# Moving the fetch of the next x, two centred tiles and the splitting units in a hand-ordered retention and FFN kernel

## The chip, the core and the metric

The kernel runs on one core of one Trainium2 chip. A core has five engines with a queue each: TensorE (PE, matmuls; its weight loads are listed as PEld), VectorE (DVE), ScalarE (ACT), GpSimd (POOL) and SyncE (SP, which here issues nearly all DMAs). Each works through its queue in order and waits for the others by semaphores. The metric is the device time of one execution in microseconds; lower is better.

## The reference

Input x has 4 sequences of 1024 tokens with 512 features. Two sublayers follow one another, each with a layer norm before it and one after it, and added to its input:

```python
def attn(x):                                   # x is already normed
    q = x @ Wq.T;  v = x @ Wv.T                # 512 x 512 each
    ret = scan(v)                              # state = lam * state + v_t along the tokens, lam per head
    out = layernorm(q * ret) * gamma + beta
    return (out * silu(x @ Wg.T)) @ Wo.T

def ffn(x):                                    # weights rounded to fp8, I = 1536
    return ((silu((x @ gate_w) * gate_scale) * ((x @ up_w) * up_scale)) @ down_w) * down_scale

x = x + layernorm(attn(layernorm(x)))
x = x + layernorm(ffn(layernorm(x)))
```

All is in float32, and the kernel keeps that precision: operands are either multiplied as float32 or split into parts [...].

## The kernel before

The 4096 tokens are worked in 8 blocks of 512 tokens (t = 0 to 7), a block in 4 tiles of 128 tokens (s = 0 to 3). The main loop (line 1223) runs over blocks, and within a block over 12 steps (line 1226, i = 0 to 11), one for each 128 of the 1536 hidden columns. Every step holds the FFN of block t: `f.gate(i)` (8 matmuls into pfg, read by ACT), `f.up(i)` (8 matmuls into pfu), `f.fuse(i)` (DVE's gate product, then ACT's cast), `f.rest(i)` one step later (DVE), and `f.down(i - 2)` (8 matmuls into pd). Gate and up share two PSUM banks in turn, so that up(i+1) waits until DVE has read up(i).

Between these, by hand, stand three other pieces of work: `l`, the FFN before, being normed and stored (steps 2 to 4); `b`, the attention of block t+1; and `n`, the preparation of block t+2 (an object `Retention`, made at the end of step 4). Every engine's order is the order of the program text (class InOrder, line 66), so where a call stands in the loop body decides behind what it queues on its engine. Within a step the body runs, from line 1228 to 1541: before the gate, between gate and up, after fuse ("mid" below, around line 1381), and after down ("end", around line 1531).

Attention of a block comes in two kinds. Blocks 2 and 3 (`fast`) use seven products instead of eight of half-sized operands for each of v, q, g and o (`product`, line 650; `order`, line 333). Blocks 4 to 7 (`by_parts`) split x and the weights into a top and a low part and use three passes for v, q and g (`begin`, `end`, lines 590 and 597, placed by `gaps`, line 458), and products for o. The weights of all these are not held: they stream through a ring of four slots, and after each product or pass one fetch of 256 KB is issued on SP for the unit four places on (`fetch_weights`, line 435).

What the change touches:

- Preparing x of block t+2, for by_parts blocks (n.t = 4 to 7, so t = 2 to 5). Tile s is normed (`norm_x`, line 504, ACT), transposed in blocks of 32 (DVE) and written to DRAM (`send_x`, line 523, SP): tile 0 at the end of step 6, 1 and 2 at the end of step 7, 3 at the mid of step 8. It is read back in the wanted layout by four DMAs a tile (`fetch_x`, line 539): tile 0 in step 7, 1 to 3 in step 8. Then `low_of` (line 555: two DVE operations, top and low) and `diff_of` (line 570: one) make the parts: low 0 in step 8, low 1 and 2 in step 9 before up, diff 0, 1 and 2 in step 9 mid, low 3 and diff 3 in step 10 mid. The first use on PE is `n.gap(-2)` in step 11 (line 1340): the top pass, then the low pass, which needs the low parts of all four tiles.
- The second norm of block t+1 (`b`). The o products give mids; `o_moments` (statistics on DVE, rstd on POOL), `x1_of` (line 901: three ACT operations, POOL's addition to x, a store), `x1_moments`, `x1n_of` (line 912: centre and scale). Tiles 0 and 1 are centred in step 9 (lines 1360 to 1366), by DVE for blocks 2 and later (`center_scale`, line 273), and transposed by DVE and DMAs (`move_x1n`); tiles 2 and 3 are centred in steps 10 and 11 by DVE and transposed on PE (`turn_x1n`, lines 1494 and 1497).
- The splitting units (class Splitter, line 388), in blocks 1 and 2: twelve units of 256 KB of Wv, Wq and Wg are loaded, split by three DVE operations and one POOL operation, and the parts are stored in DRAM for the by_parts blocks. One load of two units at the end of step 0 of block 1, then one unit a step in steps 1, 3, 4, 5, 8, 9 of block 1 and 0 to 5 of block 2 (line 1227), always loading at the mid and storing at the end.
- The sums of Wo (`output_sums`, line 371; `keep_sums`, line 383) at the end of step 0 of block 1: three plain quarters are stored to DRAM, four sums made on DVE in the same place and stored.

## Time and profile before

| | before |
|---|---|
| median of 3 timed runs (range) | 990.18 us (989.87 to 992.27) |
| the profiled execution, whole | 991.58 us |
| its span, first to last instruction | 989.8 us |
| PE busy | 954.3 us (96%) |
| DVE, ACT, POOL busy | 679.1, 427.3, 273.0 us |
| mean granted TensorE clock | 0.992 |
| start of the loop's block 0, 1, 2, 3, 4, 5, 6, 7 | 94.7, 197.8, 323.4, 449.1, 568.0, 685.3, 804.5, 915.0 us |

In the profile's lines an instruction is named by engine, operation and out<-in tiles: pfg, pfu and pd are gate, up and down; pv, pq, pg and po the attention's products; pt a transpose on PE; mids the attention's sums; st and mv statistics; split_room the splitting units. An idle stretch of an engine stands in brackets with what ended it. All instructions carry one line number (L74), that of the helper that keeps the order, so they are told apart by tiles. The row of a window gives the busy time of PE, PEld, DVE, ACT and POOL with the number of instructions, then the granted TensorE clock as a share of full speed (PEclk), the DMA share and GB/s.

### The profile page before, as it was taken

Reading aid. Unit: us, or ns where it says so; the run is one execution under the profiler, and the core shown is the slowest. Engines: PE = TensorE matmul, PEld = TensorE weight load, DVE = VectorE, ACT = ScalarE, POOL = GpSimd, SP = SyncE. Lnnn points to the kernel's source line nnn. Section 1 sums busy time; section 2 is a strip of 40 time slices with the busy share of each in tenths; the row PEclk is TensorE's granted clock in tenths of the full one; section 3 lists DMA queues with packets and bytes.
Section 4 is the critical chain, followed back from the end, with each engine's and each line's share of the span. In section 5 each row is a group of like instructions: output and inputs, shape, how many; then the busy total and the mean of one; then the engine's idle time right before and its main releaser. Section 6 shows DMA issues by size and latency. Waiting matters only on the chain.

```text
span 989.8 us, 11929 instructions
## 1 busy us (share of the span) xinstructions
PE 954.3 (96%) x4022; PEld 748.0 (76%) x4022; DVE 679.1 (69%) x1054; ACT 427.3 (43%) x673; POOL 273.0 (28%) x340
## 2 busy tenths in 40 slices
PE   9999999999999999989999899998999999999997
PEld 7456766777877878768878688886878778788885
DVE  5996998767768788674675845867457755647444
ACT  3546674467555125332353324433163332624223
POOL 1405212404327043140332305222052311414020
PEclk9999999999999999999999999999999999999999
DMA  9312324864738557455455465455454454424021
GB/s 296 119 64 69 123 65 111 268 200 153 226 116 244 177 171 261 153 155 179 150 170 155 128 186 149 162 156 177 144 174 153 135 181 145 148 64 125 4 86 42
DMA packets 115500, 148.14 MB, mean 150 GB/s; under 512 B 10864, under 2 KB 60016, under 8 KB 115440
## 3 DMA queue, kind: packets, MB, share of 16 engines
q1 hardware_dynamic: 114576, 146.73, 47.8%
q8 instruction: 32, 0.52, 0.3%
q10 hardware_dynamic: 864, 0.66, 0.2%
q14 instruction: 28, 0.23, 0.1%
HBM read 108.02 MB, written 42.47 MB: 152 GB/s over the span
## 4 chain that ended last, share of the span: by engine, by line
PE 38%; DVE 8%; POOL 4%; ACT 3%; issue 3%; DMA 1%; SPq 0%; DVEq 0%; POOLq 0%; ACTq 0%
PE pd L74 8%; PE pfg L74 8%; PE pfu L74 8%; PE pv L74 4%; PE po L74 4%; PE pq L74 3%; PE pg L74 2%; DVE st L74 2%; DMA kept<-x 1%; POOL x L74 1%; POOL d L74 1%; ACT x1n L74 1%; DVE diff L74 1%; DVE low L74 1%; POOL mvd L74 1%
## 5 line engine op out<-in xcount | busy, mean ns | idle before, releaser
L74 PE MATMUL pfu<-x1nT,up_sb 128*128 128x512 f32 x768 | 201.6, 405 | 5.5 <-DVE gate L74 5.5
L74 PE MATMUL pfg<-x1nT,gate_sb 128*128 128x512 f32 x768 | 194.7, 395 | 0.1
L74 PE MATMUL pd<-down_sb,fuse 128*128 128x512 f32 x720 | 186.0, 400 | 0.0
L74 PEld LDWEIGHTS pfu<-x1nT,up_sb 128*128 128x128 f32 x768 | 144.6, 189 | 41.0 <-DVE gate L74 8.6
L74 PEld LDWEIGHTS pfg<-x1nT,gate_sb 128*128 128x128 f32 x768 | 144.0, 188 | 30.4 <-DVE x1nT L74 0.8
L74 PEld LDWEIGHTS pd<-down_sb,fuse 128*128 128x128 f32 x720 | 136.8, 190 | 28.5
L74 ACT CAST fuse<-gate 128x512 fp32r<-128x512 f32 x90 | 55.6, 618 | 183.5 <-DVE gate L74 183.5
L74 DVE SCALAR_TENSOR_TENSOR gate<-pfu,us_sb,gate 128x512 f32<-128x512 f32 x96 | 71.8, 748 | 59.6 <-PE pfu L74 53.6
L74 ACT ACTIVATE gate<-pfg,gs_sb 128x512 f32<-128x512 f32 x96 | 65.6, 684 | 105.4 <-PE pfg L74 105.3
L74 POOL TENSOR_SCALAR mv<-mv 128x1 f32<-128x1 f32 (+1 forms) x82 | 23.8, 290 | 253.0 <-DVE mv L74 249.9
L74 DVE TENSOR_TENSOR fuse<-gate,fuse 128x512 fp32r<-128x512 f32 x90 | 73.9, 821 | 5.5 <-ACT fuse L74 5.5
L74 DVE BATCH_NORM_STATS2 st<-x 128x6 f32<-128x512 f32 x64 | 43.6, 681 | 25.3 <-POOL x L74 22.6
L74 POOL TENSOR_TENSOR ysum<-y 128x512 f32<-128x512 f32 (+1 forms) x10 | 12.0, 1202 | 156.8 <-DVE y L74 156.7
L74 POOL TENSOR_TENSOR mv<-mv,nhalf 128x1 f32<-128x1 f32 (+1 forms) x75 | 50.9, 679 | 6.2
L74 DVE TENSOR_TENSOR mids<-po,mids 128x512 f32<-128x512 f32 x30 | 20.5, 684 | 36.4 <-PE po L74 36.3
L74 POOL TENSOR_TENSOR x<-x,x1n 128x512 f32<-128x512 f32 x32 | 41.5, 1298 | 12.7 <-ACT x1n L74 12.0
L74 POOL TENSOR_TENSOR d<-d,x 128x512 f32<-128x512 f32 x28 | 36.2, 1317 | 16.1 <-ACT d L74 14.1
L74 POOL TENSOR_TENSOR sqsum<-sqsum,sq 128x512 f32<-128x512 f32 x24 | 35.1, 1464 | 14.9 <-ACT sq L74 13.5
L74 POOL TENSOR_TENSOR ysum<-ysum,y 128x512 f32<-128x512 f32 (+1 forms) x20 | 23.1, 1157 | 54.3 <-DVE y L74 54.0
L74 DVE TENSOR_TENSOR y<-pq,y 128x512 f32<-128x512 f32 x18 | 12.4, 691 | 35.7 <-PE pq L74 35.7
L74 POOL TENSOR_SCALAR split_room<-split_room 128x512 f32<-128x512 f32 x12 | 9.5, 788 | 93.2 <-DVE split_room L74 93.2
L74 DVE RECIPROCAL rstd<-rstd 128x512 f32<-128x512 f32 x8 | 26.8, 3352 | 11.8 <-ACT rstd L74 11.8
(199 smaller groups left out, 1636.6 us busy)
## 6 DMA issues: line engine op xcount, KB each, us to landing
kept<-x SPq DMA_DIRECT2D x32, 256.0 KB, 2.1
x<-kept SPq DMA_DIRECT2D x32, 256.0 KB, 4.3
x<-in_x SPq DMA_DIRECT2D x28, 256.0 KB, 4.5
w_ring_parts<-dsum_o SPq DMA_DIRECT2D x28, 256.0 KB, 2.7
out<-d SPq DMA_DIRECT2D x27, 256.0 KB, 2.0
xnT<-mx SPq DMA_DIRECT2D x64, 64.0 KB, 2.0
w_ring_parts<-dtop_v SPq DMA_DIRECT2D x16, 256.0 KB, 2.9
w_ring_parts<-dlow_v SPq DMA_DIRECT2D x16, 256.0 KB, 2.9
```

The costliest lines, as they stand in the source:

```text
L74: return lambda *args, **kwargs: tc.keep_in_program_order(op(*args, **kwargs))
```

## The change

Seven edits, all in where things stand:

1. For by_parts blocks, x tile 1 is normed and sent in step 7 before up, tile 2 at the mid of step 7 and tile 3 at the end of step 7. The fetch is by pairs: tiles 0 and 1 in step 7 mid, tiles 2 and 3 in step 8 before up.
2. low 0 and 1 move to step 8 before up, low 2 and 3 to the end of step 8.
3. diff 0 and 1 move to step 9 before up, diff 2 and 3 to step 10 mid, after x1n of tile 2.
4. x1n of tiles 0 and 1 in step 9 is centred on ACT (`shift_scale`, line 276: two operations on one column, one on the tile) in every fast block, so for t = 1 to 6.
5. The splitting units get a table of load (l), split (s) and store (k) by block, step and place. Units 0 to 4 are split in block 1 (steps 2, 3, 4, 8, 9), 5 to 11 in block 2 (two in step 0, two in step 1, one each in steps 2, 3, 4); none in step 5. Unit 7 uses another buffer.
6. The plain quarters of Wo are no longer stored and read back: products of blocks 2 and 3 fetch them from the input, and at the end of step 10 of block 1 they are copied from DRAM to DRAM for the later blocks.
7. The four sums of Wo are stored at the end of step 1 of block 1 instead of step 0, and the first two unit loads follow there.

```diff
@@ -370,16 +370,23 @@
 
     def output_sums():
 
+        v = woT.rearrange("(c p) f -> p c f", p=P)
+        operands["o"] = {1: v[:, 0:2, 0:H], 2: v[:, 2:4, 0:H], 3: v[:, 2:4, H:D]}
         b11, b12, b21, b22 = (wo_sb[:, i : i + 2, o : o + H] for i in (0, 2) for o in (0, H))
-        operands["o"] = {}
-        made["o"] = {1: b11, 2: b21, 3: b22}
-        keep_sums("o")
         made["o"] = {5: b11, 7: b12, 6: b22, 4: b21}
         dve.tensor_tensor(b11, b12, b11, ALU.subtract)
         dve.tensor_tensor(b12, b22, b12, ALU.subtract)
         dve.tensor_tensor(b22, b22, b11, ALU.subtract)
         dve.tensor_tensor(b21, b21, b22, ALU.subtract)
 
+    def copy_output_weights():
+
+        operands["late o"] = dict(operands["o"])
+        for j in (1, 2, 3):
+            t = dram.tile([P, 2, H], F32, tag=f"sum_o{j}", name=f"dcopy_o{j}", bufs=1)
+            sp.dma_start(t, operands["o"][j])
+            operands["late o"][j] = t
+
     def keep_sums(k):
         for j, t in made[k].items():
             operands[k][j] = dram.tile([P, 2, H], F32, tag=f"sum_{k}{j}", name=f"dsum_{k}{j}", bufs=1)
@@ -389,44 +396,51 @@
         def __init__(self):
-            self.room = wpool.tile([P, 4, D], F32, tag="wo_sb", name="split_room")
+            room = wpool.tile([P, 4, D], F32, tag="wo_sb", name="split_room")
+            self.pairs = [(room[:, 0], room[:, 1]), (room[:, 2], room[:, 3])]
...
-            self.loaded = self.done = self.kept = 0
-
-        def of(self, n):
+            self.pair = {n: p if p is None else self.pairs[p] for n, p in enumerate((0, 1, 0, 1, 0, 1, 0, None, 1, 0, 1, 0))}
+
+        def load(self, n):
...
+            if self.pair[n] is None:
+                room = work.tile([P, 2, D], F32, tag="xn", name=f"split_room_{n}", bufs=1)
+                self.pair[n] = room[:, 0], room[:, 1]
...
+        times = {
+            (1, 1, "end"): "l0 l1", (1, 2, "mid"): "s0", (1, 2, "end"): "k0", (1, 3, "mid"): "l2 s1",
+            (1, 3, "end"): "k1", (1, 4, "mid"): "l3 s2", (1, 4, "end"): "k2", (1, 5, "mid"): "l4",
+            (1, 8, "mid"): "s3", (1, 8, "end"): "k3", (1, 9, "mid"): "l5 s4", (1, 9, "end"): "k4",
+            (1, 10, "mid"): "l6", (2, 0, "mid"): "l7 s5", (2, 0, "end"): "k5 s6", (2, 1, "mid"): "l8 s7 k6",
+            (2, 1, "end"): "l9 s8", (2, 2, "mid"): "k7 k8 s9", (2, 2, "end"): "l10 k9", (2, 3, "mid"): "l11 s10",
+            (2, 3, "end"): "k10", (2, 4, "mid"): "s11", (2, 4, "end"): "k11",
+        }
+
+        def at(self, *when):
+            do = {"l": self.load, "s": self.split, "k": self.store}
+            for what in self.times.get(when, "").split():
+                do[what[0]](int(what[1:]))
@@ -443,7 +457,8 @@
         ring = rings[n >= change].bitcast(F32)[:, n % RING]
         what = stream[n]
         if len(what) == 2:
-            unit = operands[what[0]][what[1]]
+            k, j = what
+            unit = operands["late o" if k == "o" and n >= change else k][j]
             sp.dma_start(ring.rearrange("p (c f) -> p c f", c=2), unit)
         else:
             sp.dma_start(ring, operands[what[:2]][what[2]])
@@ -538,7 +553,7 @@
 
         def fetch_x(self, s=None):
             xnT = self.xnT.bitcast(F32)
-            tokens, groups = (slice(None), slice(None)) if s is None else (ts(s, P), ts(s, P // Q))
+            tokens, groups = (slice(None), slice(None)) if s is None else (ts(s, 2 * P), ts(s, 2 * P // Q))
             for a in range(NQ):
                 sp.dma_start(
                     xnT[ts(a, Q), groups].rearrange("p g c j -> p g (c j)"),
@@ -1224,7 +1239,6 @@
         f, n = Ffn(a), None
         fast = b is not None and b.fast
         for i in range(NI):
-            splits = (t == 1 and i in (1, 3, 4, 5, 8, 9)) or (t == 2 and i < 6)
             if t > 0 and (t > 1 or i) and not (fast and i == 11):
                 (f if i else l).rest((i - 1) % NI)
             if t == 0 and i == 0:
@@ -1272,9 +1286,16 @@
                 b.gap(3 * i)
             if fast and 7 <= i < 10:
                 b.product()
-            if n and n.by_parts and i in (8, 9):
-                for s in ([0], [1, 2])[i - 8]:
-                    n.low_of(s)
+            if n and n.by_parts and i == 7:
+                n.norm_x(1, True)
+                n.send_x(1)
+            if n and n.by_parts and i == 8:
+                n.fetch_x(1)
+                n.low_of(0)
+                n.low_of(1)
+            if n and n.by_parts and i == 9:
+                n.diff_of(0)
+                n.diff_of(1)
             if t == PARTS - 2 and i == 9:
                 for _ in range(RING - 1):
                     fetch_weights()
@@ -1354,19 +1375,14 @@
                 n.input_sums(*((3, 4) if fast else (1, 2)))
             if t == 0 and i == 11:
                 b.upper_of(2)
-            if n and n.by_parts and i == 9:
-                n.diff_of(0)
-                n.diff_of(1)
             if fast and i == 9:
                 loads = []
                 for s in range(2):
-                    b.x1n_of(s)
+                    b.x1n_of(s, shift_scale)
                     loads.append(b.move_x1n(s))
                 for load in loads:
                     load()
-                if n and n.by_parts:
-                    n.diff_of(2)
-                elif n:
+                if n and not n.by_parts:
                     n.input_sums(1, 2)
             if fast and i == 11:
                 for s in range(2):
@@ -1378,9 +1394,6 @@
                 next(passing)
             if fast and i < 6:
                 b.gap(3 * i + 1, 2 if i == 1 else 1)
-            if splits:
-                splitter.load()
-                splitter.split()
             if fast and i == 2:
                 l.stats(1)
             if fast and i == 3:
@@ -1400,18 +1413,20 @@
                 b.gate_y(0)
                 b.gate_y(1)
                 b.y_sums(1, 2)
-            if n and n.by_parts and i == 8:
-                n.fetch_x(1)
-                n.fetch_x(2)
-            if n and t > 0 and i == 8:
+            if (1, 0) < (t, i) < (2, NI):
+                splitter.at(t, i, "mid")
+            if n and t > 0 and i == 8 and not n.by_parts:
                 n.norm_x(3, True)
                 n.send_x(3)
             if n and n.by_parts and i == 7:
                 n.fetch_x(0)
             if fast and i in (7, 8):
                 b.product()
-            if n and t > 0 and i == 8:
-                n.fetch_x(3 if n.by_parts else None)
+            if n and n.by_parts and i == 7:
+                n.norm_x(2, True)
+                n.send_x(2)
+            if n and t > 0 and i == 8 and not n.by_parts:
+                n.fetch_x()
             if fast and i == 8:
                 b.o_moments(0)
                 b.o_moments(1)
@@ -1423,10 +1438,9 @@
             if fast and i == 10:
                 b.x1_moments(2)
                 b.x1_moments(3)
-                if n and n.by_parts:
-                    n.low_of(3)
                 b.x1n_of(2)
                 if n and n.by_parts:
+                    n.diff_of(2)
                     n.diff_of(3)
             if t == 0:
                 if i == 3:
@@ -1455,7 +1469,7 @@
             if b and not fast and i >= 9:
                 b.rest_of(i - 9)
             if n and t > 0 and i in (6, 7):
-                for s in ([0], [1, 2])[i - 6]:
+                for s in ([0], [3] if n.by_parts else [1, 2])[i - 6]:
                     n.norm_x(s, True)
                     n.send_x(s)
             for _ in range(look[i][1] if t == 1 else 0):
@@ -1503,6 +1517,9 @@
                 b.gap(3 * i + 2)
             if fast and i in (7, 8):
                 b.product()
+            if n and n.by_parts and i == 8:
+                n.low_of(2)
+                n.low_of(3)
             if fast and i == 2:
                 l.stats(2)
             if fast and i == 3:
@@ -1524,12 +1541,13 @@
                 n.stats(1)
             if t == 1 and i == 0:
                 output_sums()
+                splitter = Splitter()
+            if t == 1 and i == 1:
                 keep_sums("o")
-                splitter = Splitter()
-                splitter.load()
-                splitter.load()
-            if splits:
-                splitter.store()
+            if t == 1 and i == 10:
+                copy_output_weights()
+            if (1, 0) < (t, i) < (2, NI):
+                splitter.at(t, i, "end")
             if t == 0 and i == 10:
                 t_sums = wpool.tile([P, 4, 2, H], F32, tag="wq_sb", name="t_sums")
                 mids = wpool.tile([P, 4, 2, H], F32, tag="wg_sb", name="mids")
```

More of the change, by code (lines that the diff above doesn't have):

```diff
@@ L398, in of @@
+        def load(self, n):
             k, c = self.units[n]
-            w, top = self.room[:, 2 * (n % 2)], self.room[:, 2 * (n % 2) + 1]
-            return k, c, w, top
-        def load(self):
-            n = self.loaded
-            if n < len(self.units) and n - self.kept < 2:
-                self.loaded += 1
-                k, c, w, _ = self.of(n)
-                src = self.sources[k].rearrange("(c p) f -> p c f", p=P)[:, :, ts(c, P)]
-                sp.dma_start(w.rearrange("p (c f) -> p c f", c=NC), src)
-                parts = operands[k, c] = {
-                    part: dram.tile([P, D], F32, tag=f"{part}_{k}{c}", name=f"d{part}_{k}{c}", bufs=1)
-                    for part in ("top", "low", "diff")
-                }
-                sp.dma_start(parts["top"].rearrange("p (c f) -> p c f", c=NC), src)
@@ L415, in split @@
-        def split(self):
-            if self.done < self.loaded:
-                _, _, w, top = self.of(self.done)
-                dve.tensor_scalar(top.bitcast(I32), w.bitcast(I32), TOP_MASK, None, ALU.bitwise_and)
-                dve.tensor_tensor(w, w, top, ALU.subtract)
-                dve.scalar_tensor_tensor(top, top, -LOW, w, ALU.mult, ALU.add)
-                pool.tensor_scalar(w, w, 1.0 / LOW, 1.0, ALU.mult, ALU.mult)
-                self.done += 1
-        def store(self):
-            while self.kept < self.done:
-                k, c, w, top = self.of(self.kept)
-                sp.dma_start(operands[k, c]["diff"], top)
-                sp.dma_start(operands[k, c]["low"], w)
-                self.kept += 1
+            if self.pair[n] is None:
+                room = work.tile([P, 2, D], F32, tag="xn", name=f"split_room_{n}", bufs=1)
+                self.pair[n] = room[:, 0], room[:, 1]
@@ new lines, in load, with split @@
+            w = self.pair[n][0]
+            src = self.sources[k].rearrange("(c p) f -> p c f", p=P)[:, :, ts(c, P)]
+            sp.dma_start(w.rearrange("p (c f) -> p c f", c=NC), src)
+            parts = operands[k, c] = {
+                part: dram.tile([P, D], F32, tag=f"{part}_{k}{c}", name=f"d{part}_{k}{c}", bufs=1)
+                for part in ("top", "low", "diff")
+            }
+            sp.dma_start(parts["top"].rearrange("p (c f) -> p c f", c=NC), src)
+        def split(self, n):
+            w, top = self.pair[n]
+            dve.tensor_scalar(top.bitcast(I32), w.bitcast(I32), TOP_MASK, None, ALU.bitwise_and)
+            dve.tensor_tensor(w, w, top, ALU.subtract)
+            dve.scalar_tensor_tensor(top, top, -LOW, w, ALU.mult, ALU.add)
+            pool.tensor_scalar(w, w, 1.0 / LOW, 1.0, ALU.mult, ALU.mult)
@@ L431, in retention_ffn_sandwich, with store @@
+        def store(self, n):
+            (k, c), (w, top) = self.units[n], self.pair[n]
+            sp.dma_start(operands[k, c]["diff"], top)
+            sp.dma_start(operands[k, c]["low"], w)
+        times = {
[6 rows of a table added]
+        }
+        def at(self, *when):
+            do = {"l": self.load, "s": self.split, "k": self.store}
+            for what in self.times.get(when, "").split():
+                do[what[0]](int(what[1:]))
     RING = 4
```

## The prediction, made before the result was seen

> **What bounds the kernel now.** I read the page's totals, the list of waits by engine, a count of where each step starts, and then the timeline of the stretches that stood out.

> ```profile
> PE 954.3 (96%) x4022; PEld 748.0 (76%) x4022; DVE 679.1 (69%) x1054; ACT 427.3 (43%) x673; POOL 273.0 (28%) x340
> ```

> TensorE (PE) is busy 954.3 of 989.8 us, and no matmul is removed. So the change can only win PE's idle time, and the slow matmuls that idling brings.

> ```profile
> PE pv L74 <- DVE low L74: 8.6, 4, 2.4
> PE pfu L74 <- DVE gate L74: 5.5, 5, 1.3
> PE po L74 <- issue: 3.7, 2, 1.8
> PE pq L74 <- DMA w_ring<-dsum_q: 1.7, 1, 1.7
> ```

> Columns: us in all, times, longest. I took a step to last from its first gate matmul (pfg) to that of the next step, in the timeline. Step 11 of blocks 2 to 5 takes 14.89, 16.46, 14.84 and 16.82 us, with 3.3 to 3.7 idle in each. Step 7 takes 14.37 in block 1 and 14.25 in block 2, but 10.46 in blocks 3 to 6, which run the same matmuls. These are the places. Step 11 of block 3 in the timeline (start, length, engine):

> ```profile
> 554.79 2.11 PE L74 MATMUL pfu<-x1nT,up_sb 128*128 128x512 f32 x8 [1.27 <-DVE gate L74]
> ...
> 559.16 0.69 DVE L74 TENSOR_TENSOR low<-xnT,top 128x512 fp32r<-128x512 f32 x1
> ...
> 559.91 1.20 PE L74 MATMUL pv<-low,w_ring_parts 128*128 128x512 f32 x4 [2.06 <-DVE low L74]
> ...
> 560.94 3.58 PE L74 MATMUL pd<-down_sb,fuse 128*128 128x512 f32 x8
> ```

> PE waits 1.27 us for VectorE (DVE) to read the previous up product, because DVE is four microseconds behind its queue; then 2.06 us for low(3), which stands in DVE's queue behind statistics that wait for GpSimd's x1. Then eight down matmuls take 3.58 us instead of the 1.99 of block 2. The windows say why:

> ```profile
> 443.00:446.00 3.00, 3.00 (x17) 2.49 (x16) 2.83 (x6) 2.14 (x4) 0.06 (x1) 1.00 0.38 94
> ...
> 561.00:564.40 3.40, 3.40 (x10) 2.51 (x9) 2.93 (x5) 2.14 (x4) 0.00 (x0) 0.50 0.32 82
> ```

> PEclk is third from the end: 0.50 for 3.4 us after the wait. The same follows the two waits of 1.8 us in step 7 (277.7 and 400.5) and the wait of 2.4 in block 5 (796.5). Blocks 2 and 4 wait 2.06 too and keep 1.00. The four slow windows begin whole multiples of 3.413 us apart (36, 47 and 69), as if on a clock of their own; on that grid the waits of blocks 2 and 4 fall into two windows (0.9 + 1.15, 0.3 + 1.75), the other four into one.

> Step 7 of block 2:

> ```profile
> 389.40 0.69 DVE L74 SCALAR_TENSOR_TENSOR split_room<-split_room 128x512 f32<-128x512 f32 x1
> ...
> 399.38 1.41 DVE L74 SCALAR_TENSOR_TENSOR y<-y,lnb_sb,mids 128x512 f32<-128x512 f32 x2
> ...
> 400.22 3.54 PE L74 MATMUL po<-w_ring,y 128*128 128x256 f32 x8 [1.83 <-issue]
> ```

> The wait is booked as issue, but PE starts just as the first of the two y's is gated. DVE has no gap from the splitting unit of step 5 (388.2 to 390.1) to there. Block 1 is the same.

> **The change, part by part.** Sums are against the profiled execution: 991.58 us, of which 989.8 is the span; the median of the three timed runs, 990.18, lies 1.4 below it.

> Splitting units. A unit is three DVE operations (0.42 + 0.69 + 0.69 = 1.8 us), one on GpSimd and four DMAs. Step 5 loses its unit in blocks 1 and 2. That brings the gating of y forward by 1.8 us and by another 0.35, as one scaling of y was stretched from 0.74 to 1.10 beside the unit's GpSimd operation: 2.15 against a wait of 1.83. I leave 0.3 per block for the second y. Gain: 14.37 - 10.46 - 0.3 = 3.6 and 14.25 - 10.46 - 0.3 = 3.5, half-clock windows included, 7.1 together.

> [...] The rows show the drop after 1.8 us, if one window holds the whole gap. [...]

> The units go elsewhere. Block 1 gets one in step 2, as block 2 has now; block 2's step 3 takes 11.41 against block 1's 9.79, so 1.6 is lost. Block 2 gets four in steps 0 and 1 instead of two, 3.6 us more DVE work. Its waits for PE there (0.40, 2.36, 1.01, 0.35, 0.91) cover most; what is left, some 0.9, reaches the product at 359.96, which already waits 0.13 for DVE: 1.0 lost. Bounds for both: 0 to 5. Four unit DMAs hold SP some 2 us (0.4 to 0.6 each), two units in one step 4 us; the weight fetches behind them have the ring's lead, about 14 us (next paragraph), and without it would cost what the late one cost at 226.03, 1.7.

> Output weights. Now SP issues seven stores back to back:

> ```profile
> 209.68 6.58 SPq L74 DMA_DIRECT2D dsum_o<-wo_sb x7
> ```

> and then waits for them before two unit loads, so that the fetch of the weights that PE lacks at 226.03 goes out only at 220.69. Three stores go, four move to the end of step 1 together with the loads and their copies. There the queue is held some 6.3 us (four stores 2.1, landing 2.0, four loads 2.2), and the next weight fetches stand behind it; but they are issued four products ahead, about 14 us. So the 1.67 goes, and the 0.65 at 216.97, where DVE's sums wait 1.3 us for those stores: 2.3. Reading three of the seven units in rows of 1 KB from the input costs nothing visible: such reads of wvT land in 3.8 us against 3.4 for stored sums, inside the same lead. The three copies late in step 10 of block 1 take about 1.7 us of SP behind the stores of x1; only weight fetches with the ring's lead stand behind them; without it, 1.7 once.

> Next x. low(3) leaves step 10, and all low parts are ready by about 542 (they start when DVE has added the o product of the end of step 8, 539.7, and take 2 x 1.12), 15 us before PE asks. The wait of 2.06 is gone. The price: norm and transpose of tile 1 stand before DVE's gate product of step 7, the two low parts (2.2 us) before that of step 8; the banks they free are wanted over 6 us later (531.5 and 542.2). low(2) and low(3) stand before rest(8), which PE wants at 549.7 and gets at 542.6. Were these covers gone, each would cost its own 1 to 2 us. On SP, eight fetches of 128 KB replace sixteen of 64 KB, each some 0.43 to issue, 3.5 us saved; the first pair waits for tile 1's landing and holds the weight fetch behind it 2.3 us, inside the ring's lead. xnT lands by 529 and 536, wanted at 532.6 and 539.7.

> Two x1n tiles on ScalarE (ACT).

> ```profile
> L74 DVE TENSOR_SCALAR x1n<-x,mv x25: 504/540/1506, 193.5 to 911.4; 128x512 f32<-128x512 f32 x25
> L74 ACT ACTIVATE x1n<-mids,nb,mv x24: 812/816/819, 298.9 to 906.9; 128x512 f32<-128x512 f32 x24
> ```

> [...] DVE gives up 2 x 0.54 = 1.1 us, ACT takes 2 x 1.44 (two short ones of 0.2 and 0.3, then 0.82) = 2.9, and ACT can start only after casting fuse(9). [...] In blocks 2 to 5, I get for block 3: gate product of step 9 done at 546.9 (547.7 before, since diff(0), diff(1) move ahead of it and low(1), low(2) went), cast 547.5, tiles 549.0 and 550.4, transposes done 551.15, so the o statistics begin at 551.1 instead of 551.8. Then up(11) starts at about 554.05 instead of 554.79, and x1n(3), at the end of the chain of statistics, GpSimd additions and again statistics, is ready at 561.0 instead of 562.0. PE now gets to its transpose at 559.95 and waits there 1.1: this is what is late next. Transposed at 563.22 (block 2's time carried over) before, at 561.1 after: 2.1 won per block, not 3.3. Four blocks: 8.4. With a longest single wait of 1.1 no half-clock window is left, so step 11 of blocks 3 and 5 also loses its 1.6 and 2.0: 3.6.

> In blocks 1 and 6 nothing is relieved in exchange. Block 1: DVE gets the second tile 1.0 later, of which 0.2 comes back, as the unit behind it no longer runs beside GpSimd's t_sums (0.70 instead of 0.42 for its first operation): 0.8 lost. Block 6: the chain moves from 903.3 to 905.3; x1n(3) at 913.9 against a transpose at 912.7: 1.3 lost.

> Sum: -7.1 - 2.3 - 8.4 - 3.6 + 1.6 + 1.0 + 0.8 + 1.3 = -16.7. 991.6 - 16.7 = 974.9; if the median again lies 1.4 below its profile, 973.5. I say 974.5.

> **Rivals.** (a) The likeliest, as summed: 970 to 980, chance 0.55. (b) No wait follows: up(11) does not wait 0.55, the transpose does not wait 1.1 (4 x 1.65 = 6.6), and the extra units are covered (2.6): 974.9 - 9.2, about 966, chance 0.17. For it: DVE is only 60% busy in blocks 3 to 5. Against: the chain that ended last runs through exactly these statistics. (c) One of the two step 7 waits stays (3.5) and step 11 gains 1.2 instead of 2.1 (3.6): 982, chance 0.18. (d) The change doesn't do what it says: each wait is replaced by one as long, 988 to 991, chance 0.05. (e) Slower: the ACT detour. DVE's o statistics stand behind two transposes that stand behind ACT; if they start d later than I place them, up(11) and x1n(3) are d later in each of blocks 1 to 6. From d about 1.25 the wait at up(11) passes 1.8 and each block pays a half-clock window of 1.7 too: 6 x (1.25 + 1.7) = 17.7, more than the 16.7 won. With d = 2: 974.9 + 22, about 997. For it: ACT's gate(10) stands behind the tiles, 0.4 before gate(11) wants its bank. Against: ACT is 43% busy and idle 5 us before that cast. Chance 0.05.

> Measured, 0.3% (3 us) can be told from no change. Range 966 to 984: (a) whole, most of (b) and (c). Faster by over 0.3% 0.91, within 0.04, slower 0.05.

> **What would show it.** Right: no PE wait on low; step 11 of blocks 2 to 5 near 12.8, with a wait of pt for x1n near 1 us; step 7 near 10.8 in blocks 1 and 2; PEclk 1.00 from 5 us to the last matmul; step 11 of block 6 near 9.4; block 2's step 3 above 11.4. Wrong: po still waiting in step 7, a new wait on xnT's DMA under low, or PE's gate(11) waiting for ACT.

## The result and the profile after

| | before | after |
|---|---|---|
| median, runs of one chip taken in turn (range) | 990.18 us (988.88 to 992.27) | 984.96 us (984.02 to 987.1) |
| ratio after / before, 95% interval | | 0.9949 [0.9931, 0.9967] |
| span of the profiled execution | 989.8 us | 983.1 us |
| mean granted TensorE clock | 0.992 | 0.997 |

The change gains 0.5%, 5.2 us, where 15.7 were forecast; 984.96 lies 1 us above the range. First the totals of the changed kernel and its list of waits (us in all, times, longest), the same two views as in the prediction:

```profile
PE 952.1 (97%) x4022; PEld 746.2 (76%) x4022; DVE 681.0 (69%) x1042; ACT 442.2 (45%) x709; POOL 270.8 (28%) x340
...
PE pfu L74 <- DVE gate L74: 7.1, 9, 1.4
PE pg L74 <- ACT mids L74: 5.8, 2, 2.9
PE pt L74 <- DVE x1n L74: 3.7, 7, 1.2
```

All three waits that the change aimed at are gone: none on low, none of po in step 7, none on the weight ring. But a pair of new ones stands there, pg on ACT's mids, 2.9 us each; before had one such wait, of 0.6. The timeline of PE has the stretches that the prediction read (step 7 of block 2, step 11 of block 3), and the new wait:

```profile
251.84 2.67 PE L74 MATMUL pg<-t_sums,w_ring 128*128 128x256 f32 x8 [2.90 <-ACT mids L74]
...
401.26 2.02 PE L74 MATMUL po<-w_ring,y 128*128 128x256 f32 x8
...
554.02 2.14 PE L74 MATMUL pfu<-x1nT,up_sb 128*128 128x512 f32 x8 [0.95 <-DVE gate L74]
...
556.94 1.07 PE L74 MATMUL pv<-low,w_ring_parts 128*128 128x512 f32 x4
```

Measured as in the prediction, from a step's first gate matmul to the next step's, the steps say where the time went. The last column is run e4 of the next section, with two parts of the change corrected.

| steps (us) | before | after | both corrected |
|---|---|---|---|
| 1 and 2 of block 1 | 13.33, 12.58 | 12.39, 10.66 | 12.39, 10.66 |
| 2 of block 2 | 10.66 | 12.14 | 12.14 |
| 3 of blocks 1, 2 | 9.79, 11.41 | 11.00, 10.04 | 10.49, 10.02 |
| 4 of blocks 1, 2 | 12.07, 11.21 | **15.93, 14.32** | 11.86, 11.85 |
| 7 of blocks 1, 2 | 14.37, 14.25 | 10.61, 10.64 | 10.60, 10.60 |
| 10 of blocks 2 to 5, sum | 22.18 | **25.94** | 24.83 |
| 11 of blocks 2 to 5, sum | 63.01 | 51.92 | 45.71 |
| 11 of block 1 | 12.78 | 13.68 | 12.91 |
| 11 of block 6 and 0 of block 7 | 13.76 | 15.37 | 13.76 |

**Step 4.** Block 1 in the timeline, before and then after:

```profile
244.72 2.54 POOL L74 TENSOR_TENSOR d<-d,x 128x512 f32<-128x512 f32 x2
244.75 2.48 DVE L74 TENSOR_TENSOR y<-y,mu 128x512 f32<-128x512 f32 x4 [0.59 <-PE mu L74]
...
249.54 0.67 ACT L74 ACTIVATE gate<-pfg,gs_sb 128x512 f32<-128x512 f32 x1
```

```profile
243.07 3.11 POOL L74 TENSOR_TENSOR d<-d,x 128x512 f32<-128x512 f32 x2 [1.45 <-ACT d L74]
243.37 1.67 DVE L74 TENSOR_TENSOR split_room<-split_room 128x512 f32<-128x512 f32 x1
...
245.08 1.65 DVE L74 SCALAR_TENSOR_TENSOR split_room<-split_room 128x512 f32<-128x512 f32 x1
...
246.65 2.47 DVE L74 TENSOR_TENSOR y<-y,mu 128x512 f32<-128x512 f32 x4
...
250.63 0.67 ACT L74 ACTIVATE gate<-pfg,gs_sb 128x512 f32<-128x512 f32 x1
```

Before, y - mu starts 0.2 us after PE's gate(4) (244.55); after, 3.3 us after it (243.39). The unit of step 3, which stood ahead of the halves, now stands between them and y - mu, and two of its operations take 1.67 and 1.65 us beside GpSimd's additions of d; in step 4's unit, with no addition beside it, the same two take 0.69 each (256.48 and 257.21). ACT squares y, GpSimd adds the squares, ACT's last square waits for it, and ACT's gate(4) and the copy of pg stand behind that square. PE needs that copy's bank.

**Step 10.** Block 3 after; the two low parts stand at the end of step 8:

```profile
537.74 1.29 POOL L74 TENSOR_TENSOR x<-x,x1n 128x512 f32<-128x512 f32 x1 [0.33 <-ACT x1n L74]
538.08 1.24 DVE L74 TENSOR_SCALAR top<-xnT 128x512 int32<-128x512 int32 x1
...
539.21 1.27 POOL L74 TENSOR_TENSOR x<-x,x1n 128x512 f32<-128x512 f32 x1 [0.18 <-ACT x1n L74]
539.35 1.68 DVE L74 TENSOR_TENSOR low<-xnT,top 128x512 fp32r<-128x512 f32 x1
...
546.92 2.11 PE L74 MATMUL pfu<-x1nT,up_sb 128*128 128x512 f32 x8 [0.48 <-DVE gate L74]
```

The prediction had 0.42 and 0.69 for such a pair. Each of the two ends 0.3 to 0.55 us after the GpSimd operation beside which it began (539.03 and 540.48). The second pair, after GpSimd has ended, takes 0.41 and 0.69. So the four last 4.0 us instead of 2.2. The gate product of step 9 is late by about as much, up(10) waits 0.48 for it, and step 10 grows by 0.94 in the mean (a wait in brackets counts from the modelled end of the matmul before and so shows less than the start is late). Not all of that is the low parts': where they are stretched but the two tiles are centred on VectorE (e3, e4, e8 below), step 10 takes 6.20, 0.65 more than before; with the tiles on ScalarE alone (e9) it takes 5.82, 0.28 more: PE's gate(11) then starts that much later after the down matmuls ahead of it, as it waits for ScalarE's gate.

### The profile page after: what moved, and what is told of

The parts are those of the page before. It is cut to its first block, busy times and chain, and to the rows that moved or that the text cites. A ratio compares the mean times of both kernels' runs of the same rounds, so it can differ in the third digit from the quotient of the medians.

```text
span 983.1 us, 11900 instructions
## 1 busy us (share of the span) xinstructions
PE 952.1 (97%) x4022; PEld 746.2 (76%) x4022; DVE 681.0 (69%) x1042; ACT 442.2 (45%) x709; POOL 270.8 (28%) x340
## 4 chain that ended last, share of the span: by engine, by line
PE 63%; DVE 18%; ACT 7%; POOL 5%; issue 4%; DMA 3%; SPq 0%; DVEq 0%; POOLq 0%; ACTq 0%
PE pfg L74 11%; PE pfu L74 10%; PE pd L74 10%; PE pv L74 8%; PE po L74 8%; PE pq L74 8%; PE pg L74 6%; DVE st L74 3%; ACT x1n L74 2%; DVE split_room L74 2%; DVE y L74 2%; DVE fuse L74 2%; DVE gate L74 1%; POOL x L74 1%; DVE scr L74 1%
## 5 line engine op out<-in xcount | busy, mean ns | idle before, releaser
L74 PE MATMUL pfu<-x1nT,up_sb 128*128 128x512 f32 x768 | 200.7, 403 | 7.1 <-DVE gate L74 7.1
L74 PE MATMUL pfg<-x1nT,gate_sb 128*128 128x512 f32 x768 | 195.4, 396 | 0.9 <-DVE x1nT L74 0.4
L74 PE MATMUL pd<-down_sb,fuse 128*128 128x512 f32 x720 | 184.8, 398 | 0.0
L74 PEld LDWEIGHTS pfu<-x1nT,up_sb 128*128 128x128 f32 x768 | 143.6, 188 | 43.1 <-DVE gate L74 10.9
L74 PEld LDWEIGHTS pfg<-x1nT,gate_sb 128*128 128x128 f32 x768 | 143.7, 188 | 32.9 <-ACT gate L74 2.1
L74 PEld LDWEIGHTS pd<-down_sb,fuse 128*128 128x128 f32 x720 | 136.1, 189 | 28.1
L74 ACT CAST fuse<-gate 128x512 fp32r<-128x512 f32 x90 | 55.7, 619 | 198.7 <-DVE gate L74 198.6
L74 ACT ACTIVATE gate<-pfg,gs_sb 128x512 f32<-128x512 f32 x96 | 65.6, 683 | 96.5 <-PE pfg L74 96.5
L74 DVE SCALAR_TENSOR_TENSOR gate<-pfu,us_sb,gate 128x512 f32<-128x512 f32 x96 | 71.6, 745 | 51.5 <-PE pfu L74 47.2
L74 POOL TENSOR_SCALAR mv<-mv 128x1 f32<-128x1 f32 (+1 forms) x82 | 24.3, 297 | 273.7 <-DVE mv L74 270.6
L74 DVE TENSOR_TENSOR fuse<-gate,fuse 128x512 fp32r<-128x512 f32 x90 | 74.7, 830 | 5.5 <-ACT fuse L74 5.5
L74 DVE BATCH_NORM_STATS2 st<-x 128x6 f32<-128x512 f32 x64 | 43.6, 681 | 24.8 <-POOL x L74 22.2
L74 POOL TENSOR_TENSOR ysum<-y 128x512 f32<-128x512 f32 (+1 forms) x10 | 11.8, 1183 | 171.2 <-DVE y L74 171.2
L74 POOL TENSOR_TENSOR mv<-mv,nhalf 128x1 f32<-128x1 f32 (+1 forms) x75 | 50.2, 670 | 6.2
L74 POOL TENSOR_TENSOR x<-x,x1n 128x512 f32<-128x512 f32 x32 | 41.5, 1296 | 12.3 <-ACT x1n L74 12.0
L74 POOL TENSOR_TENSOR d<-d,x 128x512 f32<-128x512 f32 x28 | 37.1, 1348 | 18.6 <-ACT d L74 16.7
L74 DVE TENSOR_TENSOR mids<-po,mids 128x512 f32<-128x512 f32 x30 | 20.5, 684 | 28.7 <-PE po L74 28.4
L74 POOL TENSOR_TENSOR sqsum<-sqsum,sq 128x512 f32<-128x512 f32 x24 | 34.9, 1454 | 17.4 <-ACT sq L74 16.0
L74 DVE TENSOR_TENSOR y<-pq,y 128x512 f32<-128x512 f32 x18 | 12.5, 692 | 37.4 <-PE pq L74 37.4
L74 POOL TENSOR_TENSOR ysum<-ysum,y 128x512 f32<-128x512 f32 (+1 forms) x20 | 22.2, 1110 | 52.1 <-DVE y L74 51.8
L74 DVE RECIPROCAL rstd<-rstd 128x512 f32<-128x512 f32 x8 | 26.8, 3352 | 11.5 <-ACT rstd L74 11.4
L74 ACT ACTIVATE scr<-scr,neg_low 128x1024 f32<-128x1024 f32 x18 | 20.6, 1145 | 24.1 <-DVE scr L74 24.0
```

Of the source, the lines that this page charges most:

```text
L74: return lambda *args, **kwargs: tc.keep_in_program_order(op(*args, **kwargs))
```

## The experiments

My theory: two things ate the gain, the unit's new place in step 3, and the stretched low parts; and ScalarE's tiles are a loss that the other edits hide. The rivals are in the expectations. Ratios are to runs of the kernel before on the same chip, whose median was 990.6, 992.2 and 990.89 us in the three groups; so runs of different groups are compared by ratio.

| run | median us | ratio [95% interval] |
|---|---|---|
| after | 984.96 | 0.9949 [0.9931, 0.9967] |
| e1_mid_back | 978.65 | 0.9870 [0.9848, 0.9892] |
| e2_unit_after_centre | 977.6 | 0.9861 [0.9842, 0.9880] |
| e3_x1n_on_dve | 972.91 | 0.9816 [0.9796, 0.9835] |
| e5_low_beside_act | 977.75 | 0.9865 [0.9846, 0.9883] |
| e4_both | 968.85 | 0.9764 [0.9747, 0.9781] |
| e6_low2_earlier | 966.45 | 0.9736 [0.9718, 0.9754] |
| e7_units_alone | 985.58 | 0.9931 [0.9912, 0.9949] |
| e8_next_x_alone | 975.98 | 0.9836 [0.9817, 0.9855] |
| e9_act_alone | 995.12 | 1.0041 [1.0030, 1.0051] |
| e10_unit8_later | 966.26 | 0.9750 [0.9732, 0.9769] |

**e1: the mid call back at its old place** (some twenty lines up, before the halves).

```diff
             if fast and i < 6:
                 b.gap(3 * i + 1, 2 if i == 1 else 1)
+            if (1, 0) < (t, i) < (2, NI):
+                splitter.at(t, i, "mid")
...
-            if (1, 0) < (t, i) < (2, NI):
-                splitter.at(t, i, "mid")
```

> The changed kernel with one edit: the splitting units' mid call stands where the old splitting lines stood, ahead of step 3's halves of block t+1. My theory: step 4 of blocks 1 and 2 became 3.9 and 3.1 us longer (15.93 and 14.32) because the unit of step 3 now runs on VectorE between the halves and the subtraction y - mu, beside GpSimd's additions of d, so that squares and then ACT's gate(4) come late. Put back, step 4 returns to about 12.1 and 11.2, the two PE waits of 2.9 us on mids are gone, and block 2's step 3 goes back up by about 1.4, block 1's by 0.4: about -5 us against the changed kernel, 980. Rival: the wait in step 4 comes from the number of units in blocks 1 and 2, wherever they stand in the step: step 4 stays 14 to 16 us, 984 to 986.

Measured 978.65. Step 4 is 11.21 in both blocks, the waits for pg are gone, step 3 is 12.52 and 11.40. The place is the cause of what step 4 lost; the number of units is not. Block 1's new unit still costs 2.7 in step 3 (9.79 before). Of that 1.23 is a wait of PE for a q product's sum, which stands on VectorE behind the unit, and the unit starts late because its load has not landed:

```profile
232.06 0.43 DVE L74 TENSOR_SCALAR split_room<-split_room 128x512 int32<-128x512 int32 x1 [1.83 <-DMA split_room<-in_wvT]
```

**e2: the unit of step 3 behind y - mu.** The entries of the table that change:

```diff
-            (1, 3, "mid"): "l2 s1", (1, 3, "end"): "k1", (1, 4, "mid"): "l3 s2",
+            (1, 3, "mid"): "l2", (1, 3, "end"): "s1", (1, 4, "mid"): "k1 l3 s2",
...
-            (2, 3, "mid"): "l11 s10", (2, 3, "end"): "k10", (2, 4, "mid"): "s11",
+            (2, 3, "mid"): "l11", (2, 3, "end"): "s10", (2, 4, "mid"): "k10 s11",
```

> The changed kernel, but the units of step 3 of blocks 1 and 2 are split at the end of step 3, behind the subtraction y - mu, and stored in step 4 mid. My theory (only the place ahead of y - mu hurts): step 4 is about 12 and 11 us, step 3 stays near 11.0 and 10.0 or gets shorter; -7 us against the changed kernel, 978. Rival (DVE has too much to do in steps 3 and 4 wherever the unit stands): the unit delays what follows in step 4 and no more than 2 us come back, 983 or above.

Measured 977.6. Step 3 is 10.12 and 10.01, step 4 is 11.86 and 11.85. Block 1 in the timeline:

```profile
242.16 2.48 DVE L74 TENSOR_TENSOR y<-y,mu 128x512 f32<-128x512 f32 x4 [0.59 <-PE mu L74]
...
245.84 1.67 DVE L74 TENSOR_TENSOR split_room<-split_room 128x512 f32<-128x512 f32 x1
```

The unit is stretched here too, but behind y - mu it costs little: against e1, step 4 takes 0.65 more and step 5 0.36 more (9.32 against 8.96). So the stretch costs where something that PE needs soon stands behind it.

**e3: x1n of tiles 0 and 1 back on VectorE**, which undoes edit 4 alone.

```diff
-                    b.x1n_of(s, shift_scale)
+                    b.x1n_of(s)
```

> The changed kernel, but x1n of tiles 0 and 1 is centred on VectorE as before, in one operation of 0.54 us each, so that only the ScalarE part of the change is undone. My theory: the detour over ScalarE lets the o statistics of tiles 2 and 3 begin 1.6 us later than VectorE alone would (4.15 us after the gate product instead of about 2.5), with the diffs already moved away: blocks 1 and 6 win 0.9 and 1.6 back, blocks 2 to 5 about 1.3 to 1.6 each, 7 to 9 us in all: 976 to 978. Rival (the idea of the change, that VectorE is relieved at the right place): undoing it costs about 1 us in each of blocks 2 to 5, 988 or more.

Measured 972.91, 12 less than after; more than expected. Between the two profiled spans it is 11.0. Steps 10 and 11 of blocks 2 to 5 together go from 19.46 to 17.61, 1.85 each; block 1 wins 0.7 in step 11, blocks 6 and 7 win 1.6. That is 9.7. PE's wait for the q product's sum in block 1's step 3 (the one of e1) is 0.73 in the profile of after, 0 here and in e2 and e5, and 0.15 to 0.4 in e4, e6 and e10: 0.9 of the 11.0 is such scatter. It comes from the unit's load: edit 7 issues it 29.5 us after the start of block 1 (20.4 before), it lands 2.9 to 4.9 us later, and where it lands late VectorE waits for it (1.29 in after, nothing here). First after, then e3, from the gate product of step 9 on:

```profile
546.11 0.75 DVE L74 SCALAR_TENSOR_TENSOR gate<-pfu,us_sb,gate 128x512 f32<-128x512 f32 x1
548.89 0.71 DVE L74 STREAM_TRANSPOSE xs<-x1n 128x512 f32<-128x512 f32 x1 [2.03 <-ACT x1n L74]
...
551.00 0.65 DVE L74 BATCH_NORM_STATS2 st<-mids 128x6 f32<-128x512 f32 x1
```

```profile
542.21 0.75 DVE L74 SCALAR_TENSOR_TENSOR gate<-pfu,us_sb,gate 128x512 f32<-128x512 f32 x1
542.88 0.54 DVE L74 TENSOR_SCALAR x1n<-x,mv 128x512 f32<-128x512 f32 x1
...
545.26 0.65 DVE L74 BATCH_NORM_STATS2 st<-mids 128x6 f32<-128x512 f32 x1
```

From the start of the gate product to the o statistics (those of the o product's tiles 2 and 3) it is 4.89 us with ScalarE's tiles and 3.05 with VectorE's own: 1.84 later, almost the 1.85 that steps 10 and 11 lose.

**e5: low(2) and low(3) into that wait of 2.03**, with ScalarE's tiles kept.

```diff
+            if n and n.by_parts and i == 9:
+                n.low_of(2)
+                n.low_of(3)
             if fast and i == 9:
                 loads = []
...
-            if n and n.by_parts and i == 8:
-                n.low_of(2)
-                n.low_of(3)
```

> The changed kernel, but low(2) and low(3) go from the end of step 8 to step 9 between the gate product and the transposes, where VectorE waits 2.03 us for ScalarE's tiles and GpSimd does nothing. My theory: the four operations took 4.0 us at the end of step 8 (the first pair 1.24 and 1.68 instead of 0.42 and 0.69) because GpSimd adds x at that time; in the new place they take 0.42 and 0.69 each, the gate product of step 9 comes earlier, PE's waits at up(10) (0.48) and gate(11) (0.28) go, and step 10 of blocks 2 to 5 goes back from 6.49 to about 5.55: -3.7, with up to 2 more from the shorter wait for x1n in step 11; 979 to 981. Rival: step 10 is long because ScalarE's gate(10) stands behind the two centred tiles, whatever VectorE does before: step 10 stays at 6.4 to 6.5, 984 to 986; and if low is slow in itself, the four operations take 4 us there too and step 11 gets longer.

Measured 977.75, a little better than expected. Step 10 is 5.44 in blocks 2 to 5, step 11 is 12.44. The gate product of step 9 now ends 97.7 us after the start of the block, where the prediction had it, and the wait at up(11) is 0.56. The four operations take 0.42, 0.69, 0.42, 0.69. In their old place now stands rest(8), and takes 1.49 instead of 0.69: the stretch moves on, but to one operation. The rival (ScalarE's gate(10) makes step 10 long whatever VectorE does before) falls, as ScalarE's order is the same.

**e4: e2 and e3 together.**

> The changed kernel with both corrections: units of step 3 split behind y - mu, and x1n of tiles 0 and 1 centred on VectorE. My theory: the two losses lie in different blocks' steps (3 and 4 of blocks 1 and 2; 9 to 11 of blocks 1 to 6) and add up: 984.96 - 7.4 - 12.0 = 965.6, 964 to 967. Rival: they share something (the same half-clock windows, the same waits), and the sum is well short: 970 or more.

Measured 968.85, on a chip where the kernel before took 992.2; by the ratio, 0.9764 x 990.18 = 966.8, inside what was expected. The two losses add up. It beats both kernels.

**e6: e4 with low(2) ahead of the o product's sum.**

```diff
+            if n and n.by_parts and i == 8:
+                n.low_of(2)
             if fast and i in (7, 8):
                 b.product()
             if n and n.by_parts and i == 8:
-                n.low_of(2)
                 n.low_of(3)
```

> As the run with both corrections, but low(2) goes ahead of the o product's sum at the end of step 8, into the 1.12 us in which VectorE waits for PE and GpSimd does nothing; low(3) stays. My theory: the first pair then costs 1.1 in an idle stretch instead of 2.9, only low(3) is stretched beside GpSimd, the gate product of step 9 comes 1.1 us earlier, PE's wait of 0.46 at up(10) goes and step 10 of blocks 2 to 5 shrinks from 6.20 to about 5.45: -3 against the run with both corrections, 962 to 963. Rival: the stretch only moves to whatever VectorE runs beside GpSimd's additions, or the sum of the o product comes late: no gain, 965 to 967.

Ratio 0.9736, 2.8 us under e4 by the ratios, 3.7 between the profiled spans. Step 10 is 5.44 to 5.46. In block 3 the two low parts stand on either side of the start of GpSimd's additions:

```profile
526.23 0.43 DVE L74 TENSOR_SCALAR top<-xnT 128x512 int32<-128x512 int32 x1
...
526.69 0.69 DVE L74 TENSOR_TENSOR low<-xnT,top 128x512 fp32r<-128x512 f32 x1
...
527.77 2.71 POOL L74 TENSOR_TENSOR x<-x,x1n 128x512 f32<-128x512 f32 x2
527.96 1.39 DVE L74 TENSOR_SCALAR top<-xnT 128x512 int32<-128x512 int32 x1
...
529.39 1.64 DVE L74 TENSOR_TENSOR low<-xnT,top 128x512 fp32r<-128x512 f32 x1
```

The same two operations on the same kind of tile: short without the additions, 1.0 longer each beside them. That, with e5, is the test of the stretch by itself.

**e7: edits 5 to 7 alone**, on the kernel before, with the mid call at the old place.

> The kernel before with edits 5 to 7 alone (table of splitting units, Wo), the mid call at its old place. My theory: step 7 of blocks 1 and 2 gives 7.4, the Wo stores 2.9, and steps 2 and 3 of blocks 1 and 2 take 3 back: 983 (982 to 984.5). Rival: the gain in step 7 needs the rest of the change: 988 or more.

Ratio 0.9931, or 983.3 us of 990.18. Step 7 is 10.61 in both blocks, as in after: this gain needs nothing else.

**e8: edits 1 to 3 alone**, on the kernel before.

> The kernel before with edits 1 to 3 alone (next x), x1n of tiles 0 and 1 still centred on VectorE and the splitting units as before. My theory: steps 10 and 11 of blocks 2 to 5 come down from 85.2 us to the 70.4 of the run with x1n on VectorE, -14.8: 975.6 (974.5 to 977). Rival: the move of low and diff pays only together with ScalarE's tiles, as these take from VectorE what low adds ahead of step 9's gate product: 981 or more.

Ratio 0.9836, 16.2 us of 990.18. Steps 10 and 11 of blocks 2 to 5 are as in e3 (17.6 each); the rival falls. e7 and e8 multiply to 0.9768, close to e4's 0.9764: the two groups of edits are worth 2.3% together, and edit 4 with the moved mid takes 1.8% of it back.

**e9: edit 4 alone**, on the kernel before.

> The kernel before with edit 4 alone: x1n of tiles 0 and 1 centred on ScalarE. My theory: the detour is a loss in the old order too. There diff(0) and diff(1) fill part of VectorE's wait for the tiles, so the o statistics come about 0.9 us later (not 1.6) in blocks 2 to 5, and up(11) and low(3) with them: 4 x 0.9 = 3.6; blocks 1 and 6 lose 0.8 and 1.6: +6 against the kernel before, and up to 1.6 more for each of the four waits at up(11) (1.27 + 0.9) that falls into one half-clock window: ratio 1.006 to 1.012. Rival: in the old order VectorE is the queue that is late, and taking 1.1 us of work from it gains: 0.996 to 1.000.

Ratio 1.0041: the detour is a loss in the old order too, but a smaller one than I expected. Steps 10 and 11 of blocks 2 to 5 sum to 89.15 against 85.19, of which some 1.6 is one more half-clock window (three against two); 2.3 is left, 0.6 a block, where I had 0.9. (Its profile also has no half-clock window in step 7, 12.74 and 12.75 against 14.37 and 14.25, though the waits of 1.82 and 1.83 are the same; that is no doing of the edit.) The same edit costs 1.85 a block in the new order. The difference is in what VectorE has to do while ScalarE centres: here two diffs (1.28 us) stand between the gate product and the transposes, and the o statistics come 0.64 later than before, not 1.84.

**e10: e6 with unit 8 behind the q product's sum.**

```diff
-            (2, 1, "end"): "l9 s8", (2, 2, "mid"): "k7 k8 s9", (2, 2, "end"): "l10 k9", (2, 3, "mid"): "l11",
+            (2, 1, "end"): "l9", (2, 2, "mid"): "k7 s8", (2, 2, "end"): "k8 l10 s9", (2, 3, "mid"): "k9 l11",
```

> As the run with low(2) earlier, but unit 8 of block 2 goes from the end of step 1 to the mid of step 2, and unit 9 from there to the end of step 2. My theory: PE's wait of 1.20 for the sum of a q product in block 2's step 2 comes from unit 8, which stands on VectorE 2.2 us ahead of that sum: the wait goes and step 2 returns from 12.13 to 10.66, -1.4, ratio about 0.972. Rival: the units are then late for something else in steps 2 and 3 (the y sums, or the next load): no gain, 0.9736 or more.

Ratio 0.9750, not to be told from e6. Step 2 of block 2 is 10.66 as expected, and step 3 is 11.87 instead of 10.04, with a wait of 1.5 us of mu for ACT's half. The rival holds: units 8 and 9 cost 1.5 to 1.8 us in both places tried.

## Why the prediction was wrong

**Right.** What bounds the kernel, and where its waits stood. Step 7: -7.1 forecast, 14.37 + 14.25 - 10.61 - 10.64 = -7.4 measured. Wo's stores: -2.3, and -2.9. Step 11 of block 1: +0.8, and +0.9. Block 6 (with the next step): +1.3, and +1.6. Step 11 of blocks 2 to 5: -12.0, and -11.1, with all half-clock windows there gone, as forecast. Inside that step the waits are not those of the forecast: 0.95 at up(11), where 0.55 was forecast, and 0.4 at the transpose, where 1.1 was.

**Near by luck: the other units.** Block 1's step 3 was to lose 1.6 and lost 1.2; block 2's steps 2 and 3 together were to lose 1.0 and lost 0.1. But "block 2's step 3 above 11.4", a sign of being right, did not come: it is 10.04, because the unit there has left its place ahead of the halves, and step 2 loses 1.48. With the mid call where the forecast had it (e1), block 1's step 3 loses 2.7 and block 2's two steps 1.5. Of the 2.7, 1.2 is the wait behind the unit's load, which the forecast put at nothing; the other 1.5 is near its 1.6.

**Failed: the place of the splitting units within a step, "Block 1 gets one in step 2, as block 2 has now".** The forecast counted units by step and took "mid" for one place. The new call is put at another mid, behind the halves of step 3, and I did not read which calls of the body lie between the two places. It forecast nothing for step 4 and got 3.86 + 3.11 = +7.0; in block 1 this holds a half-clock window (at 253.0), where the forecast had none. e1 and e2 show that the place is all of it: either correction brings step 4 back to 11.2 to 11.9. As the same move shortens step 3, its net price is less, 5.7 between the profiled spans of after and e1. I had gone through SP's queue for what the moved unit passes, and not through VectorE's.

**Mis-sized: "they start when DVE has added the o product of the end of step 8, 539.7, and take 2 x 1.12".** The start was right; the length was 4.0 us and not 2.24, so the gate product of step 9 ended 1.5 us later in its block than I placed it (99.26 us after the block's start instead of 97.8). up(10) waits 0.48, and step 10 grows by 0.94 four times: +3.8 against 0. Some 2.6 of it is this length (0.65 a block, e3). The other 1.1 goes with ScalarE's tiles: "PE's gate(11) waiting for ACT", one of the prediction's own signs of being wrong, came true, by 0.28 us a block. The row that would have told the length was in my own first part: the scaling of y at 1.10 instead of 0.74 beside a GpSimd operation. I used it for a gain and not for the parts that I moved under GpSimd's additions. The rows of after show more of it: top, low and the unit end 0.3 to 0.55 us after the GpSimd operation, and y - mu is not stretched: it takes 2.48 us for four tiles beside the very additions of d in the kernel before (244.72) and 2.47 without them in after. What sets it apart, no run here shows. So the price of the stretch can be estimated beforehand from such rows, for operations like top, low and the unit's: about the rest of the GpSimd operation. Here that was 1.13 us (539.35 to 540.48) for a low that took 0.99 longer, and 1.12 and 1.10 (from 243.37 and 245.08) for two operations of the unit that took 0.98 and 0.96 longer.

**A net that hid a loss: the two tiles on ScalarE.** I had the loss from the rows, about 1.8 us a block (ACT's 2.9 less the 1.1 that VectorE gives up), in hand, and then set it against the work that edits 1 to 3 take away ahead of it; in my sum the statistics came out 0.7 earlier, and the part looked harmless. In the run they came 0.7 later than before (103.4 us after the start of the block, against 102.7), as the stretched low parts had delayed the gate product. The total of step 11 was not far off, but e3 and e8 show that the relief came from edits 1 to 3 alone. Without edit 4 step 11 gains 17.3 instead of 11.1. The estimate of the loss was right: 1.85.

Sum: -7.4 - 2.9 + 1.2 + 0.1 + 7.0 - 11.1 + 3.8 + 0.9 + 1.6 = -6.8, against -6.7 between the spans. Without the two failed terms (7.0 and 3.8) it is -17.6, near the -16.7 forecast, but partly by luck: with the units' price as in e1 (2.7 and 1.5 for 1.2 and 0.1) this sum would give -14.7.

Of the rivals, (c) has the nearest number (982) by another way: both waits of step 7 went. (d) has its wrong number, but it describes half of what happened: the two waits of step 7 (1.82 and 1.83) went, and two of 2.9 came in step 4. (e), the ScalarE detour, has a d that counts from a start that already holds the detour. By that measure d was 1.4 us in blocks 2 to 5 (103.4 for 102.0), and it came from the gate product, late by 1.5, not from ScalarE, whose part took 4.1 us as forecast (4.2); what the detour itself costs is the 1.84 of e3. PE was late too by then, so up(11) waits 0.95, and none of the half-clock windows that (e) feared came there.

## What to carry to other kernels

Where every engine keeps the order of the text, a call moved by a few lines is a change of its own: list what now stands between its old and its new place on each engine, and who waits for that. Cost an edit both alone and in the order that the other edits leave: the same two tiles cost 0.6 us a block while VectorE had other work to do meanwhile, and 1.85 once that work stood elsewhere. Before work is moved on VectorE, look at what GpSimd does at that time: here top and low took 1.24 and 1.68 us beside its additions, and 0.41 and 0.69 behind them.

## What the runs showed of the hardware

```profile
274.25:277.66 3.41, 1.58 (x7) 0.82 (x6) 3.38 (x6) 2.06 (x4) 1.48 (x4) 1.00 0.00 0
277.66:281.07 3.41, 3.41 (x9) 2.70 (x9) 3.38 (x4) 2.23 (x4) 2.60 (x2) 0.50 0.02 7
677.03:680.44 3.41, 1.66 (x7) 1.39 (x8) 3.23 (x8) 0.43 (x1) 1.92 (x3) 1.00 0.58 181
680.44:683.85 3.41, 3.41 (x21) 2.91 (x20) 3.24 (x7) 2.80 (x6) 0.00 (x0) 1.00 0.23 77
```

So waits of one length came at different prices. In after, the wait of 2.9 us for pg in step 4 of block 1 put 2.23 us of idle PE into one window; that of block 2 was parted, 1.33 and 1.53, and no drop followed. Block 1's is 2.90, 2.89 and 2.89 us in after, e3 and e5, whose work up to there is the same, and it brought one window at half clock, none and two: step 4 takes 15.93, 14.30 and 17.14. (In e5 the first of the two, from 249.7, ran at 0.50 with 0.88 us of idle PE in it, and the second followed.) The row of a window just behind that wait, after and then e3:

```profile
253.00:256.40 3.40, 3.40 (x9) 2.68 (x8) 1.85 (x3) 2.50 (x4) 2.56 (x3) 0.50 0.21 33
```

```profile
250.60:254.00 3.40, 3.40 (x15) 2.93 (x16) 1.61 (x3) 3.38 (x5) 3.40 (x3) 1.00 0.21 24
```

So a difference of 1.6 us between two kernels with such waits can be nothing more than this. And a wait that goes can give more than its length: in step 7 of block 1 a wait of 1.82 us went, and the step came down by 3.76 (14.37 to 10.61). With the wait there and no window at half clock behind it, in e9, the step took 12.74.
